# Splitting the last layer of a four-layer graph network: low nodes by buckets, high nodes by gathers

## The chip, the cores and the metric

The kernel runs on one core of a Trainium2 chip. The core has five engines that work from their own instruction streams: PE (TensorE, matmuls), DVE (VectorE), ACT (ScalarE), POOL (GpSimd, here mostly the issuer of indirect DMAs) and SP (SyncE, here the issuer of the plain DMAs). The metric is the device time of one execution in microseconds; a time is the median of several executions. A profiled execution is one more, with its own time.

## The reference, cut to what matters

There are 12500 nodes with 128 values each and 200000 edges `src -> dst`. The edges come sorted by `dst`; `dst` is drawn as 12500 times the square of a uniform number, so that low nodes have many edges and high nodes few: 121410 of the 200000 edges end in nodes below 4608. `src` is uniform. Four layers follow each other, each on a normalized copy `h` of the nodes and each added to them: an attention over all edges (layer 0), a second attention with edge weights (layer 1), and

```python
row = concatenate([src, dst]); col = concatenate([dst, src])     # layer 2: both directions
y = segment_sum(dinv[row] * dinv[col] * (h @ W)[col], row, N) + dinv**2 * (h @ W) + b

neigh = segment_sum(h[src], dst, N) / maximum(deg, 1)            # layer 3: into dst only
z = h @ W_self.T + neigh @ W_neigh.T + b
z = relu((z - mean(z, axis=0)) * rsqrt(var(z, axis=0) + 1e-5) * gamma + beta)
x = x + z
```

Layer 3 ends with a normalization over all nodes, so its mean and variance need every node's sum first.

## The kernel before, in words

Nodes lie in 98 blocks (`NB`) of 128. Tables that edges read (`zt` for layer 2, `h3` for layer 3) hold each row as two half-precision parts, 512 B, in DRAM.

The kernel sums along edges in two ways.

*By gathers.* A list holds, per edge, the row to fetch and the place in its block. `gather` (L291) issues one indirect DMA on POOL for 128 edges. A "hot" matrix, built by one DVE comparison (L1522), then adds the 128 fetched rows to their places by two matmuls (one for each part, L1524), and DVE adds the result to an accumulator (L1528). Layer 0 (`layer0_edges`, L1103) does this along `dst`, where the list needs no padding: 391 windows (`NW`) of 512 edges, each touching two neighbouring blocks, with a mask for each of the two. Its lists (`lists`, L1813) live in SBUF until layer 0 is over. Layers 1 and 2 do it along `src`, with lists padded to whole blocks: 1664 gathers each, in 416 groups of four (`sum_rows`, L1507).

*By buckets.* The second direction of layer 2, and the whole of layer 3, are summed along `dst` from edges sorted by block of `src` and, within a block, by class of `dst`. A class is `dst % 26` (`CLASSES`), its columns are `dst // 26` (`COLS` = 481, `COLS2` = 482). A bucket is one block and one class, at most 128 edges; there are 2548. `buckets` (L840) takes four classes at once (`AT_ONCE`) and walks all 98 blocks. For each block DVE builds `mine` (L867), which picks the source rows of 4x128 edges; for each bucket PE multiplies it with the block's table rows `z` (256 columns, L873), ACT copies the result `r` to half precision (L878), DVE builds `yours` (L875), the edges' columns within the class, and PE adds into the class's sums (two matmuls of 482 columns, L852). Two buckets make a step; a step's sums are added two steps later. `z` and the edges' lanes are loaded by SP for seven blocks at a time (`ZB`), in two buffers. When the four classes are through, `finish` is called for each. In layer 2 (`class_rows`, L891) it turns the sums by PE, copies them (`turned`, L904, two buffers) and stores them to the table `y` in DRAM. In layer 3 it multiplies with `W_neigh` (L1687), scales by the node's degree (`rdegk`, L1689), adds into `yt`, which holds all nodes turned (L1691), and takes the statistics (L1692).

The buckets' edges and columns are prepared beside layer 1 by `bucket_starts` (L749). It counts, for each bucket (128 in a column, `BC` = 20 columns), the edges before it, first over the first edges of all rows in five parts (L777), then within one row that it gathers (L790). It then gathers 128 edges (L805) from a view that starts at every fourth edge (`STEP`), finds which belong to the bucket and stores lanes and columns. Should a bucket not fit, `over` is set, the buckets are emptied, and loops that otherwise run no times (`sum_again`, `means_again`) gather all edges instead. The order of edges is made beside layer 0 by a sort whose keys are packed and unpacked by DVE (L373, L388).

The order of the work is that of the program, arranged by the framework within each engine's stream. In layer 2, `sum_rows` takes the bucket steps between its groups, 1300 of them over 416 groups. In layer 3 nothing but the buckets runs in the loop, with `own_parts` (`h @ W_self`, L1657) between: one of its 75 pieces at every second step. After the loop come the normalization and the output, L1698 on.

Of the kernel before, what the change touches and what calls it, by code (L numbers as in the profile page):

```python
# [36 lines left out]
P = 128  # L37
# [32 lines left out]
CLASSES = 26  # L70
COLS = -(-N // CLASSES)
COLS2 = COLS + COLS % 2
BUCKETS = NB * CLASSES
BC = -(-BUCKETS // P)

STEP = 4
# [30 lines left out]
class Net:  # L107
# [256 lines left out]
    def by_class(self, q, r, n):  # L364

        nc = self.nc
        nc.vector.tensor_scalar(q, n, 1.0 / CLASSES, 0.5 / CLASSES, op0=OP.mult, op1=OP.add)
        nc.vector.scalar_tensor_tensor(r, q, -float(CLASSES), n, op0=OP.mult, op1=OP.add)
        nc.vector.scalar_tensor_tensor(q, r, 0.0, q, op0=OP.is_ge, op1=OP.add)
        nc.vector.tensor_scalar(q, q, -1.0, None, op0=OP.add)  # L370
        nc.vector.scalar_tensor_tensor(r, q, -float(CLASSES), n, op0=OP.mult, op1=OP.add)

    def pack_buckets(self, key, own, other, more):  # L373
# [7 lines left out]
        self.by_class(own, more, other)  # L381
# [6 lines left out]
    def unpack_buckets(self, own, other, more, key):  # L388
        nc = self.nc
        ki = key.bitcast(I32)  # L390
        nc.vector.tensor_scalar(own, ki, 14, 0x3F80, op0=OP.logical_shift_right, op1=OP.bitwise_and)
        nc.vector.tensor_scalar(more, ki, P - 1, None, op0=OP.bitwise_and)
        nc.vector.tensor_tensor(own, own, more, op=OP.bitwise_or)
        nc.vector.tensor_scalar(other, ki, 7, 0x1FF, op0=OP.logical_shift_right, op1=OP.bitwise_and)
        nc.vector.tensor_scalar(more, ki, 16, 0x1F, op0=OP.logical_shift_right, op1=OP.bitwise_and)
        nc.vector.scalar_tensor_tensor(other, other, float(CLASSES), more, op0=OP.mult, op1=OP.add)

# [351 lines left out]
    def bucket_starts(self, work, take, keys, firsts, shifted, lanes, places, over):  # L749
# [6 lines left out]
        n = work.tile([P, BC], I32, name="bnum")  # L756
        nc.gpsimd.iota(n, pattern=[[P, BC]], base=0, channel_multiplier=1)
        s, k = (work.tile([P, BC], I32, name=f"b{c}") for c in "sk")
        self.by_class(s, k, n)
        nc.vector.tensor_scalar(s, s, 5, None, op0=OP.logical_shift_left)  # L760
        nc.vector.tensor_tensor(s, s, k, op=OP.bitwise_or)
# [9 lines left out]
        for h in range(5):  # L771
# [3 lines left out]
            for c in range(BC):  # L775
                below = work.tile([P, quarter], F32, name="bbelow")
# [20 lines left out]
        at = work.tile([P, BC], I32, name="bat")  # L797
        nc.vector.tensor_scalar(at, ri, int(math.log2(STEP)), None, op0=OP.logical_shift_right)
# [3 lines left out]
        for c in range(BC):  # L802
            m = min(P, BUCKETS - c * P)
            edge = work.tile([P, P], I32, name="bedge", bufs=2)
            self.gather(edge, shifted, at, c)  # L805
# [34 lines left out]
    def buckets(self, work, psum, table, lanes, place, finish):  # L840
# [14 lines left out]
        for k0 in range(0, CLASSES, AT_ONCE):  # L855
            n = min(AT_ONCE, CLASSES - k0)
            sums = [psum.tile([P, 512], F32, name=f"sums{i}", bufs=1)[:, :COLS2] for i in range(n)]
            for s in range(NB):
                if s % ZB == 0:
                    z = work.tile([P, ZB, PARTS * D], STORED, name="z", bufs=2)  # L860
                    nc.sync.dma_start(z, view[:, s:s + ZB, :])
                    lane = work.tile([P, ZB, AT_ONCE * P], F16, name="lanes", bufs=2)
                    nc.sync.dma_start(lane[:, :, :n * P], bass.AP(
                        tensor=lanes.tensor, offset=lanes.offset + (s * CLASSES + k0) * P,
                        ap=[[0, P], [CLASSES * P, ZB], [1, n * P]]))
                mine = work.tile([P, AT_ONCE * P], F16, name="mine", bufs=3)
                nc.vector.tensor_scalar(mine[:, :n * P], lane[:, s % ZB, :n * P], self.lane, None, op0=OP.is_equal)  # L867
                for i in range(0, n, 2):
                    p = psum.tile([P, 2, PARTS * D], F32, name="pout", bufs=2)
                    yours = work.tile([P, 2, COLS2], F16, name="yours", bufs=5)  # L870
                    for j in range(2):
                        b = s * CLASSES + k0 + i + j
                        nc.tensor.matmul(p[:, j, :], mine[:, (i + j) * P:(i + j + 1) * P], z[:, s % ZB, :],  # L873
                                         start=True, stop=True)
                        nc.vector.tensor_scalar(yours[:, j, :], self.iotac, place[:, b:b + 1], None,  # L875
                                                op0=OP.is_equal)
                    r = work.tile([P, 2, PARTS * D], F16, name="r", bufs=4)
# [7 lines left out]
            for i in range(n):  # L885
                o = work.tile([P, COLS2], F32, name="o", bufs=2)
# [4 lines left out]
    def class_rows(self, work, psum, out):  # L891

        nc = self.nc
        zero = work.tile([P, D], F32, name="zero")
        nc.vector.memset(zero, 0.0)
        nc.sync.dma_start(out[COLS * CLASSES:NP, :], zero[:NP - COLS * CLASSES, :])

        def finish(k, i, o):
            p = psum.tile([P, 4, P], F32, name="pout", bufs=2)
            t = work.tile([P, 4, P], F32, name="turned", bufs=2)  # L900
            for j in range(4):
                m = min(P, COLS - j * P)
                nc.tensor.transpose(p[:m, j, :], o[:, j * P:j * P + m], self.ident)
                nc.vector.tensor_copy(t[:m, j, :], p[:m, j, :])  # L904
                nc.sync.dma_start(bass.AP(tensor=out.tensor, offset=out.offset + (j * P * CLASSES + k) * D,
                                          ap=[[CLASSES * D, m], [1, D]]), t[:m, j, :])
# [28 lines left out]
    def windows(self, pool, psum, dram, lists, own, other, relb):  # L935
# [40 lines left out]
        some = pool.tile([P, 1], F32, name="somefar")  # L976
        nc.vector.tensor_reduce(some, far.rearrange("p a c -> p (a c)"), axis=AX.X, op=OP.add)
        p = self.bank(psum)
        nc.tensor.matmul(p[:, 0:1], self.ones, some, start=True, stop=True)
        nc.vector.tensor_scalar(self.sparse, p[:, 0:1], 0.5, None, op0=OP.is_gt)  # L980
# [585 lines left out]
    def layer2_edges(self, dram, zt, acc, edges, dbins, sbins, lanes, places, over):  # L1566
# [7 lines left out]
        with tc.tile_pool(name="l2a", bufs=1) as work, tc.tile_pool(name="ps22", bufs=1, space=PSUM) as psum:  # L1574
            once = self.count_of(work, over, 1)
# [35 lines left out]
    def layer3_table(self, dram, keep, x, chunks):  # L1611
# [9 lines left out]
        by_class = dram.tile([CLASSES, COLS2], F32, name="rdegc")  # L1621
        with tc.tile_pool(name="l3t", bufs=1) as pool, tc.tile_pool(name="ps3t", bufs=1, space=PSUM) as psum:
# [5 lines left out]
            t = pool.tile([CLASSES, COLS2], F32, name="rc")  # L1628
            nc.vector.memset(t, 0.0)
            nc.sync.dma_start(t[:, :COLS], bass.AP(tensor=by_node.tensor, offset=by_node.offset,  # L1630
                                                   ap=[[1, CLASSES], [CLASSES, COLS]]))
# [12 lines left out]
    def layer3(self, keep, x, table, dbins, lanes, places, over):  # L1644
# [5 lines left out]
        classes = yt.rearrange("p b e -> p (b e)")[:, :COLS * CLASSES].rearrange("p (j c) -> p j c", c=CLASSES)  # L1650
        with tc.tile_pool(name="l3a", bufs=1) as work, tc.tile_pool(name="ps33", bufs=1, space=PSUM) as psum:
            self.means_again(work, psum, yt, rdeg, ht_, dbins, over)
        st = keep.tile([P, CLASSES, 6], F32, name="bst")
        with tc.tile_pool(name="l3d", bufs=1) as work, tc.tile_pool(name="ps30", bufs=1, space=PSUM) as psum:
            place = self.bucket_places(work, places, over)

            def own_parts():  # L1657

                for lo, hi in GROUPS:
                    k = hi - lo  # L1660
                    h = work.tile([P, 4, D], F32, name="h", bufs=2)
# [4 lines left out]
                    p = psum.tile([P, 4, P], F32, name="ph")  # L1666
# [11 lines left out]
            rd = [None]  # L1678

            def finish(k, i, o):  # L1680
                if i == 0:
                    rd[0] = work.tile([P, AT_ONCE, COLS2], F32, name="rdegk")
                    n = min(AT_ONCE, CLASSES - k)
                    nc.sync.dma_start(rd[0][:, :n, :].rearrange("p k j -> p (k j)"),
                                      self.rows(by_class[k:k + n, :], n * COLS2))
                p = psum.tile([P, 512], F32, name="py")
                nc.tensor.matmul(p[:, :COLS2], self.wneigh, o, start=True, stop=True)  # L1687
                m = work.tile([P, COLS2], F32, name="m", bufs=2)
                nc.vector.tensor_mul(m, p[:, :COLS2], rd[0][:, i, :])  # L1689
                v = classes[:, :, k]  # L1690
                nc.vector.tensor_add(v, v, m[:, :COLS])  # L1691
# [3 lines left out]
            for i, _ in enumerate(self.buckets(work, psum, ht_, lanes, place, finish)):  # L1695
                if i % 2:
                    next(parts, None)
# [259 lines left out]
```

## Time and profile before

| | us |
|---|---|
| median of three timed runs | 8606.02 |
| lowest and highest of them | 8601.07 and 8621.12 |
| the profiled execution | 8595.46 |
| its span, first to last instruction | 8593.7 |
| busy in the span: PE / DVE / ACT / POOL | 6491.9 / 6414.5 / 4345.9 / 5029.4 |
| first and last start of a layer 2 gather | 4858.3 and 6984.6 |
| layer 3, from the clearing of `yt` to the last statistics | 7143.9 to 8563.65 |

In the profile, a digit in a row of slices is the busy share of one fortieth of the span (215 us) in tenths. Layer 0 takes the first ten slices, layer 1 the next twelve, layer 2 the next ten, layer 3 the last seven. A group's line names the line of the program, the engine, the operation, output and inputs, shape and count; then busy time and mean duration, and the idle time before it with what ended it. A wait's line names who waited for whom, the total in us, the number of times and the longest. In the list by time, an entry with "x4" is four instructions in a row, and the time after the first is that of all of them. Durations of matmuls overlap, so starts are better to count by than durations.

### The profile page before, as it was taken

The page shows a single profiled execution, that of the slowest core. Times are in us where ns is not written, and L with a number is a line of the kernel's source. Part 1 is how long each engine was busy: PE and PEld are TensorE (multiplying, and loading weights), DVE is VectorE, ACT ScalarE, POOL GpSimd, SP SyncE. Part 2 cuts the span into 40 slices and gives each one's busy share as a digit, 9 for nine tenths or more (in the row PEclk, how much of TensorE's full clock was granted, in tenths as well). Part 3 has the DMA queues.
Part 4 walks back from the last instruction along what each step waited for, and adds up shares of the span by engine and source line. Part 5 has one row for each costly group of instructions (what it writes and reads, how often), then busy time and mean ns, then how long its engine had stood idle before and what let it go on. Part 6 is the DMA issues. An engine that isn't in the chain of part 4 may idle for free. (4 is left out here: it accounts for less than half of the span.)

```text
span 8593.7 us, 134716 instructions
## 1 busy us (share of the span) xinstructions
PE 6491.9 (76%) x36173; PEld 4569.0 (53%) x36174; DVE 6414.5 (75%) x21784; ACT 4345.9 (51%) x8435; POOL 5029.4 (59%) x5224
## 2 busy tenths in 40 slices
PE   4455555555588988889995478888888767999999
PEld 3344444444377877778884244444444434555555
DVE  5788888887777776776777877777777776777777
ACT  4566666665455555555553333333333336555555
POOL 1777777777477777777774677777777731000000
PEclk7556655555766566665565699999999988999999
DMA  4333333333555555555553233444444443333333
GB/s 113 78 81 82 82 82 82 81 83 87 157 180 178 173 174 174 175 171 177 176 180 84 80 111 113 114 113 116 113 114 115 114 115 91 94 98 95 100 97 112
DMA packets 854249, 1021.59 MB, mean 119 GB/s; under 512 B 127765, under 2 KB 692914, under 8 KB 853232
## 3 DMA queue, kind: packets, MB, share of 16 engines
q1 hardware_dynamic: 637669, 558.29, 22.5%
q0 software_dynamic: 185728, 439.20, 18.7%
q10 hardware_dynamic: 30091, 15.25, 0.7%
q8 instruction: 319, 5.23, 0.2%
q14 instruction: 442, 3.62, 0.1%
HBM read 952.03 MB, written 60.29 MB: 118 GB/s over the span
## 5 line engine op out<-in xcount | busy, mean ns | idle before, releaser
L852 PE MATMUL sums<-yours,r 128*128 128x482 f16 x10192 | 2525.9, 372 | 219.4 <-ACT r L878 161.5
L878 ACT ACTIVATE r<-pout 128x512 f16<-128x512 f32 x2548 | 1474.0, 596 | 1941.8 <-PE pout L873 1935.9
L292 POOL DMA_INDIRECT rows<-kvt,idxs x1664 | 1618.7, 973 | 548.5 <-issue 420.9
L875 DVE TENSOR_SCALAR yours<-iotac,bucketp 128x482 f16<-128x482 f16 x5096 | 1646.1, 358 | 379.9 <-PE sums L852 379.1
L292 POOL DMA_INDIRECT rows<-zt,idxs x1664 | 1620.5, 974 | 511.2 <-issue 407.8
L292 POOL DMA_INDIRECT rows<-hw,idxd x1564 | 1489.0, 952 | 658.8 <-issue 380.9
L852 PEld LDWEIGHTS <-r 128*128 128x128 f16 x10192 | 963.2, 99 | 1032.2 <-ACT r L878 392.2
L1147 PE MATMUL psum<-rows,weights 128*128 128x130 f32 x3128 | 777.5, 419 | 589.5 <-ACT weights L1142 543.7
L1321 PE MATMUL psum<-weighted,hot 128*128 128x137 f32 x3328 | 942.8, 433 | 140.4 <-DVE acc L1323 70.7
L1147 PEld LDWEIGHTS psum<-rows,weights 128*128 128x128 f32 x3128 | 660.0, 307 | 671.5 <-ACT weights L1142 616.1
L873 PE MATMUL pout<-z,mine 128*128 128x256 f16 x5096 | 918.0, 276 | 14.1 <-DVE mine L867 9.1
L1321 PEld LDWEIGHTS psum<-weighted,hot 128*128 128x128 f32 x3328 | 732.3, 295 | 300.3 <-DVE acc L1323 196.3
L1528 DVE TENSOR_TENSOR acc<-acc,psum 128x128 f32 x1664 | 464.8, 279 | 493.7 <-PE psum L1524 487.2
L1281 ACT ACT_TABLE_LOAD x206 | 264.3, 1283 | 934.0 <-DMA near<-lengths 934.0
L873 PEld LDWEIGHTS <-mine 128*128 128x128 f16 x5096 | 478.3, 98 | 450.0 <-DVE mine L867 58.1
L1142 ACT ACTIVATE weights<-off,weight,minus 128x128 f32<-128x128 bf16 x1173 | 499.6, 483 | 386.0 <-DVE rows L1134 354.1
L1323 DVE TENSOR_TENSOR acc<-acc,psum 128x137 f32 x1664 | 486.6, 292 | 254.2 <-PE psum L1321 245.9
L1290 PE MATMUL pb<-we,near 128*128 128x8 f32 x3328 | 617.4, 322 | 3.0 <-ACT near L1281 3.0
L1290 PEld LDWEIGHTS pb<-we,near 128*128 128x128 f32 x3328 | 601.6, 279 | 20.3 <-issue 3.1
L867 DVE TENSOR_SCALAR mine<-lanes,lane 128x512 f16<-128x512 f16 (+1 forms) x1372 | 478.1, 350 | 3.1 <-PE pout L873 3.0
L1524 PE MATMUL psum<-rows,hot 128*128 128x128 f16 x3328 | 293.4, 221 | 217.7 <-DMA rows<-zt,idxs 214.5
L1316 DVE TENSOR_TENSOR weighted<-rows,weighted 128x512 f32<-128x512 f32 x416 | 271.4, 690 | 247.5 <-ACT weighted L1311 246.5
(461 smaller groups left out, 9506.2 us busy)
## 6 DMA issues: line engine op xcount, KB each, us to landing
lanes<-lanes SPq DMA_DIRECT2D x168, 896.0 KB
near<-lengths SPq DMA_DIRECT2D x208, 512.0 KB
lanes<-slanes SPq DMA_DIRECT2D x208, 256.0 KB
lanes<-dlanes SPq DMA_DIRECT2D x391, 128.0 KB
z<-zt SPq DMA_DIRECT2D x98, 448.0 KB
z<-h SPq DMA_DIRECT2D x98, 448.0 KB
rows<-kvt,idxs POOLq DMA_INDIRECT x1664
rows<-zt,idxs POOLq DMA_INDIRECT x1664
```

What stands on the lines that cost most here:

```text
L292: self.nc.gpsimd.indirect_dma_start(out=out, out_offset=None, in_=table, in_offset=bass.IndirectOffsetOnAxis(ap=idx[:, t:t + 1], axis=0))
L852: nc.tensor.matmul(sums[i], self.part(r[:, i, :], h), yours[:, i, :], start=s == 0 and h == 0, stop=s == NB - 1 and h == PARTS - 1)
L867: nc.vector.tensor_scalar(mine[:, :n * P], lane[:, s % ZB, :n * P], self.lane, None, op0=OP.is_equal)
L873: nc.tensor.matmul(p[:, j, :], mine[:, (i + j) * P:(i + j + 1) * P], z[:, s % ZB, :], start=True, stop=True)
L875: nc.vector.tensor_scalar(yours[:, j, :], self.iotac, place[:, b:b + 1], None, op0=OP.is_equal)
L878: nc.scalar.activation(r, p, AF.Copy)
L1142: nc.scalar.activation(hot[:, j, :], off, AF.Relu, bias=w[:, j:j + 1], scale=minus[:, j:j + 1])
L1147: nc.tensor.matmul(p, hot[:, j, :], rows[:, j, :n], start=j == 0, stop=j == G - 1)
L1290: nc.tensor.matmul(pb[:, j, :], hid[:, j * P:(j + 1) * P], self.we2, start=False, stop=j == W - 1)
L1321: nc.tensor.matmul(p, hot[j // G][:, j % G, :], v[:, j, :], start=True, stop=True)
L1323: nc.vector.tensor_add(d, d, p)
L1528: nc.vector.tensor_add(d, d, p[:, j, :])
```

## The change

1. There are 32 classes instead of 26, 16 (`FEW`) for nodes below 4608 (`SPLIT`) and 16 for those from 4608 on. A low class has 288 columns, a high one 496. Packing and unpacking of the sort's keys follow; there are 3136 buckets in 25 columns.
2. Layer 2 uses all 32 classes. Its `turned` tile has one buffer.
3. Layer 3's buckets are the 16 low classes only. Edges into higher nodes are gathered, from the last 155 (`LATE`) of layer 0's windows, whose lists are stored to DRAM after layer 0's preparation and loaded again in layer 3 (`late_sums`). Their sums go into an accumulator of 64 blocks from block 34 on (`BELOW` = 2 blocks of margin), which is cleared first. One late group of four gathers is taken at every fifth step, an own part at every fourth. After the loop, 16 groups of four blocks are scaled, turned, multiplied with `W_neigh` and added to `yt`, with statistics.
4. In layer 3, `z` and lanes are loaded two blocks at a time, in three buffers; `mine`, `yours`, `r`, `o`, `m`, `h` each have one buffer less, the scale row is loaded class by class into one buffer, and one PSUM tile (`py`) serves the own parts, the classes and the late groups.
5. A guard `early` joins `over`: it is set where the edge before the late windows already belongs to a node from 4608 on, or where a window was too wide.
6. A bucket's edges are read from its first edge on, not from the last multiple of four before it.

```diff
-CLASSES = 26
-COLS = -(-N // CLASSES)
-COLS2 = COLS + COLS % 2
+FEW = 16
+SPLIT = 36 * P
+CLASSES = 2 * FEW
+COLS = (SPLIT // FEW, (NP - SPLIT) // FEW)
+LATE = 155
+BELOW = 2
-STEP = 4
...
     def pack_buckets(self, key, own, other, more):
-        self.by_class(own, more, other)
+        nc.vector.tensor_scalar(own, other, int(math.log2(FEW)), None, op0=OP.logical_shift_right)
+        nc.vector.tensor_scalar(more, own, float(COLS[0]), float(FEW), op0=OP.is_ge, op1=OP.mult)
+        nc.vector.scalar_tensor_tensor(own, more, -COLS[0] / FEW, own, op0=OP.mult, op1=OP.add)
+        nc.vector.tensor_scalar(other, other, FEW - 1, None, op0=OP.bitwise_and)
+        nc.vector.tensor_tensor(more, more, other, op=OP.add)
...
     def unpack_buckets(self, own, other, more, key):
-        nc.vector.scalar_tensor_tensor(other, other, float(CLASSES), more, op0=OP.mult, op1=OP.add)
+        nc.vector.scalar_tensor_tensor(other, other, float(FEW), more, op0=OP.mult, op1=OP.add)
+        nc.vector.tensor_scalar(more, more, float(FEW), float(SPLIT - FEW), op0=OP.is_ge, op1=OP.mult)
+        nc.vector.tensor_tensor(other, other, more, op=OP.add)
...
     def bucket_starts(...):
-        at = work.tile([P, BC], I32, name="bat")
-        nc.vector.tensor_scalar(at, ri, int(math.log2(STEP)), None, op0=OP.logical_shift_right)
-            self.gather(edge, shifted, at, c)
+            self.gather(edge, shifted, ri, c)
...
-    def buckets(self, work, psum, table, lanes, place, finish):
+    def buckets(self, work, psum, table, lanes, place, finish, classes=CLASSES, zb=ZB):
+        for k0 in range(0, classes, n):
+            cols = COLS[k0 // FEW]
+                if s % zb == 0:
+                    some = 2 + (zb < ZB)
+                    z = work.tile([P, zb, PARTS * D], STORED, name="z", bufs=some)
...
     def class_rows(self, work, psum, out):
-            t = work.tile([P, 4, P], F32, name="turned", bufs=2)
+            t = work.tile([P, 4, P], F32, name="turned")
...
+    def late_sums(self, work, psum, table, lists, yt, rdeg, st):
+        acc = work.tile([P, NB - low, D], F32, name="late")
+        nc.gpsimd.memset(acc, 0.0)
+        for g in range(LATE):
+            lo = g * G
+            rows = work.tile([P, G, PARTS * D], STORED, name="rows", bufs=4)
+            for j in range(G):
+                self.gather(rows[:, j, :], table, idx, lo + j)
+            b = self.blocks_of(slot, g, 1, [DVE], NB - low - 2)
+            p = psum.tile([P, D], F32, name="psum", bufs=1)
+            for j in range(G):
+                hot = work.tile([P, P], PART, name="hot", bufs=4)
+                nc.vector.tensor_scalar(hot, self.iotac[:, :P], place[:, lo + j:lo + j + 1], None, op0=OP.is_equal)
+                for h in range(PARTS):
+                    nc.tensor.matmul(p, hot, self.part(rows[:, j, :], h), start=j == 0 and h == 0,
+                                     stop=j == G - 1 and h == PARTS - 1)
+            d = acc[:, bass.ds(b[0], 2), :]
+            for i in range(2):
+                nc.vector.scalar_tensor_tensor(d[:, i, :], p, mask[:, g, i:i + 1], d[:, i, :], op0=OP.mult, op1=OP.add)
+            yield
+        for i, (lo, hi) in enumerate(groups(SPLIT // P, NB)):
+            k = hi - lo
+            p = psum.tile([P, 512], F32, name="py")[:, :k * P].rearrange("p (b e) -> p b e", e=P)
+            for j in range(k):
+                a = acc[:, lo + j - low, :]
+                nc.scalar.activation(a, a, AF.Copy, scale=rdeg[:, lo + j:lo + j + 1])
+                nc.tensor.transpose(p[:, j, :], a, self.ident)
+            t = work.tile([P, 4, P], F32, name="hT", bufs=2)
+            nc.scalar.activation(t[:, :k], p, AF.Copy)
+            p = psum.tile([P, 512], F32, name="py")[:, :k * P].rearrange("p (b e) -> p b e", e=P)
+            nc.tensor.matmul(p, self.wneigh, t[:, :k], start=True, stop=True)
+            v = yt[:, lo:hi, :]
+            nc.vector.tensor_add(v, v, p)
+            nc.vector.bn_stats(st[:, i, :], v.rearrange("p b e -> p (b e)")[:, :min(hi * P, N) - lo * P])
+            yield
...
             def finish(k, i, o):
-                if i == 0:
-                    rd[0] = work.tile([P, AT_ONCE, COLS2], F32, name="rdegk")
+                rd = work.tile([P, COLS[0]], F32, name="rdegk")
+                nc.sync.dma_start(rd, self.rows(by_class[k:k + 1, :], COLS[0]))
...
-            for i, _ in enumerate(self.buckets(work, psum, ht_, lanes, place, finish)):
-                if i % 2:
+            sums = self.late_sums(work, psum, ht_, late, yt, rdeg, st[:, FEW:, :])
+            taken = 0
+            for i, _ in enumerate(self.buckets(work, psum, ht_, lanes, place, finish, FEW, 2)):
+                if i % 4 == 1:
                     next(parts, None)
+                while taken * 5 < i and taken < LATE:
+                    next(sums)
+                    taken += 1
+            for _ in parts:
+                pass
+            for _ in sums:
+                pass
...
+    late_lists = [dram.tile(shape, dtype, name=f"late{i}") for i, (shape, dtype) in enumerate(
+        (([P, LATE * G], I32), ([P, LATE * G], F32), ([P, LATE, 2], F32), ([1, LATE], I32)))]
+    for t, f in zip(late_lists, (lists[0][:, (NW - LATE) * G:NW * G], lists[1][:, (NW - LATE) * G:NW * G],
+                                 lists[3][:, NW - LATE:, :], lists[4][:, NW - LATE:])):
+        nc.sync.dma_start(t, f)
-    shifted = bass.AP(tensor=skeys.tensor, offset=skeys.offset, ap=[[STEP, (R + 1) * P // STEP], [1, STEP]])
+    shifted = bass.AP(tensor=skeys.tensor, offset=skeys.offset, ap=[[1, (R + 1) * P], [1, 1]])
```

## The prediction

> **What bounds the kernel now.** I read the page first (span, slices, groups), then the table by stretches for the last two layers, then the instructions in order of time inside them, then the waits. The profiled execution took 8595.46 us (span 8593.7); the median of the three timed runs is 8606.02, so 10.6 us are added at the end.
>
> The page's slices, and the two stretches of layer 2 (first line) and layer 3 (second), with time, then busy us of PE, weight load, DVE, ACT, POOL, granted clock, DMA share and GB/s:
>
> ```profile
> PE   4455555555588988889995478888888767999999
> POOL 1777777777477777777774677777777731000000
> 4900.00:6950.00 2050.00, 1644.31 (x10609) 883.91 (x10607) 1515.73 (x6364) 695.70 (x1245) 1561.48 (x1604) 0.96 0.41 115
> 7170.00:8550.00 1380.00, 1363.75 (x7777) 766.25 (x7776) 1013.40 (x3309) 804.85 (x1390) 25.12 (x20) 1.00 0.33 96
> ```
>
> Layer 3 is TensorE and nothing else: 1363.75 of 1380 us at clock 1.00, POOL idle. Layer 2 is POOL: 76% busy looks like slack, but the instructions in order of time show a gather every 1.25 us, the 0.30 us between two being "issue", with little else in it:
>
> ```profile
> 6001.24 0.94 POOL L292 DMA_INDIRECT rows<-zt,idxs  x1 [0.30 <-issue]
> 6002.49 0.94 POOL L292 DMA_INDIRECT rows<-zt,idxs  x1 [0.30 <-PE psum L1524]
> 6003.74 0.94 POOL L292 DMA_INDIRECT rows<-zt,idxs  x1 [0.30 <-issue]
> ```
>
> 1664 gathers from 4858.3 to 6984.6 make 1.279 us each, 5.11 per group of four. TensorE in that stretch works 80% (4.10 us per group) and waits 165 us for rows, so its own pace with its other waits is 92% of 5.11, 4.70 us:
>
> ```profile
> PEld L852 <- ACT r L878: 366.6, 484, 1.1
> PE psum L1524 <- DMA rows<-zt,idxs: 165.2, 147, 5.4
> PE sums L852 <- ACT r L878: 154.8, 331, 0.8
> ```
>
> The unit prices of layer 3, from the bucket loop in order of time: one step (two buckets: two gathers by matmul of 256 columns, four sums of 482) starts at 7446.21 and the next at 7447.25.
>
> ```profile
> 7446.21 0.38 PE L873 MATMUL pout<-z,mine 128*128 128x256 f16 x2
> 7446.43 0.98 PE L852 MATMUL sums<-yours,r 128*128 128x482 f16 x4
> 7447.25 0.38 PE L873 MATMUL pout<-z,mine 128*128 128x256 f16 x2
> 7447.46 0.98 PE L852 MATMUL sums<-yours,r 128*128 128x482 f16 x4
> ```
>
> That is 1.033 us for 2440 columns, 0.423 ns a column. Class groups of four end at 7400.9 and 7610.3: 209.4 us, of which 196 steps are 202.5 and the hand-over 7.
>
> **The change part by part.**
>
> *Layer 3's buckets.* 2548 buckets of 482 columns become 1568 (16 classes by 98 blocks) of 288. A step has 512+4x288=1664 columns: 0.704 us. 784 steps: 552 us. Four hand-overs: 28 us by the row above. The copies o, m and the scale rows rdegk get one buffer each, so each class's scale row can be fetched only once the one before is used; that is bounded by nothing (fetched in time) and 5 us a class (the y store below took 5 us from last copy to landing); I take 2, 32 us in all. The product that waits for the row stands on DVE ahead of the next group's selections, so PE feels it. ScalarE's copies (L878, 0.50 us apart where two follow) fit in 0.70.
>
> *Layer 3's late gathers.* 155 groups: 620 gathers by 1.279, 793 us, plus the 25 POOL additions of the own parts, 1.3 us each: 826 us of POOL. TensorE: eight 128-column matmuls a group, 0.61 us by the L1524 rows: 95 us; own parts 46 us (18.4+27.5, rows L1668 and L1673); scaling 16 matmuls, 10 us. TensorE in all: 552+60+95+46+10=763 us, 4.92 per group; with the 0.6 us of cross-waits that a group has in layer 2 (4.70-4.10) 5.5, 855 us. DVE: a step two selections of 288 and half a selection of 512 (0.26 us apart for 482, so about 0.21 and 0.26), 0.55 us, 431 in all; late 155x(4x0.16+2x0.27)=183; rest 70: 684, below both. So POOL and TensorE come out almost level, 826 and 855, and I take 870 for their meeting. Ends: 826, and 1000 (the cross-waits of 0.6 tripled, 6.5 us a group).
>
> *Its ends.* Before: the clearing of yt, 10.55 us at 7143.9, is waited for; the second clearing (64 of 98 blocks) adds 6.9. After the last gather: 5 us to land and multiply (the first gather of layer 2 took 6.7). Then 16 groups of transposes, copy, matmul, add through one PSUM buffer, which wait for the whole accumulator. The same chain for the own parts ran at 3.6 us a group with two buffers (copies at 7157.01, 7160.60, 7164.21); with one 3.8, 61 us; ends 45 and 75. Layer 3 now: 10.6+6.9+870+5+61=953 us, against 7143.9 to the last statistics at 8563.65, 1420: **-467** (-527 to -323).
>
> *Loads cut from 7 blocks to 2.* 1344 KB per seven become 384 KB per two, 196 pairs, three buffers. Layer 3 moved 115.31 MB at 32.7% of the engines in 1200 us, so full speed is 294 KB per us: 1.3 us a pair, with 210 KB of gathers 2.0 of the 4.4 us that four steps last. Two pairs ahead hide a landing up to 8.8 us. Nearest row of a landing: the first loads of layer 3 were issued at 7155.1 and used at 7166.3, 11.2 us, but with some 4 MB ahead of them. I take nothing; price in the rivals.
>
> Here the skill speaks against the change. The Trainium skill, "DMA: Bandwidth & Descriptors", section Bandwidth, says to batch transfers to 1 MiB or more, and its section Anatomy of one DMA has about 2.0 us fixed for each. By those figures a pair costs an estimated 2.9 us; hidden it changes nothing, bare it would add 196x2.9=568 us and turn the sign. No row of this case shows a bare small load.
>
> *Layer 2.* 3136 buckets for 2548; 1600 steps over the same 416 gather groups, 3.85 for 3.125. First half (288 columns): TensorE needs about 2.7 us of steps for 3.2, so POOL stays the bound, no change. Second half (496 columns, 2496 a step, 1.056 us): 3.77 bucket steps by 1.056 = 3.98 for 3.07x1.033=3.17, +0.81 a group. Work alone 4.10+0.81=4.91 still fits under 5.11; own pace 4.70+0.81=5.51 doesn't: 208x0.40=+83. That such a pace is real is seen where the gathers run out, at the end of layer 2: there the groups start 5.3 us apart with no wait for rows.
>
> ```profile
> 6994.23 0.61 PE L1524 MATMUL psum<-rows,hot 128*128 128x128 f16 x8
> 6999.52 0.61 PE L1524 MATMUL psum<-rows,hot 128*128 128x128 f16 x8
> 7004.82 0.61 PE L1524 MATMUL psum<-rows,hot 128*128 128x128 f16 x8
> ```
>
> The turned rows lose their second buffer: each class waits for the store of the one before; the third class's first copy at 5198.56 followed the first's last at 5193.2 by 5 us, waiting for that store. Three such waits at each of eight hand-overs; behind them on DVE stand the additions to acc and the next selections, which PE awaits. POOL runs seven groups ahead (35 us) and covers them inside the layer; without that cover 8x15=120 us. At the layer's end, bare, 12 us. **+95** (0 to +184).
>
> *Layer 1.* Ten more gathers (25 columns of buckets for 20, twice) on POOL, the bound there in most slices: 10x1.279=**+13** (0 to 25). DVE gets 25 more counts of 0.62 us, hidden (it is 72% busy). The gathers from the first edge on read rows of one element as start; with rows of four they took 944 ns, with rows of 128 also 944: nothing.
>
> *Layer 0 and seams.* Two more operations on 1664 columns after the sort (1.02 and 1.89 us, rows L395 and L393), between layers and bare: +3. Five operations of the packing become five. Four stores of lists, 0.36 us of SP each, ahead of the first lane loads, and four flag operations of 0.15: +1. **+4** (0 to 10). The clearings that go (rc 0.46, zero) stand beside DMA waits: nothing.
>
> Another rule against it, without use in the sum: the Trainium skill's "GPSIMD Engine Reference", section Key points, says that GpSimd shares SBUF interfaces with VectorE and contends with DVE's two-port modes. If no gather could run beside layer 3's selections, 431 us would join POOL's 826, and the time be 8250+(1257-870)=8637. The layer 2 stretch has DVE 74% and POOL 76% busy at once, and gathers of 974 ns mean against 952 in layer 0, so the trace does not show such a block.
>
> **Sum.** -467+95+13+4=-355; 8595.5-355=8240, and 10.6 up to the median: **8250 us**.
>
> **The rivals.**
> - *Bound everywhere by POOL.* Layer 3 loop 826, short tail, layer 2 unchanged: -527+0+13+4: 8096. For it: TensorE's work alone fits in both. Against: its waits for ACT r.
> - *Cross-waits in layer 3.* Every late group puts eight matmuls and two PSUM additions between the steps, on single buffers; at 6.5 us a group the loop is 1000, and layer 2 +150: 8435. For it: the 5.3 us groups above.
> - *Loads late (ends on the other side).* If pairs land 11.2 us after issue, they come 2.4 us late, 196 times: +470, 8720. It decides from 6.2 us a pair, where the loop reaches 1220. Against it: 45% load, less than layer 1's 57%.
> - *It doesn't do what it says.* If the guards fire, all edges are gathered again, over 2000 us more in each layer. By the inputs the last edge ahead of the late windows has node 4561, under 4608, and the fullest bucket 125 of 128, so they don't.
>
> **How the numbers follow.** Main case 0.70 (8130 to 8400), POOL-bound 0.13, cross-waits 0.11, loads late 0.05, guards 0.01. The range 8120 to 8440 leaves out a part of the first and the last two. A change under 0.2% (17 us) can't be told from none; only the last two are slower, about 0.01 lies between.
>
> **What would show it.** Layer 3's stretch about 950 us with POOL about 76% busy; sums of 288 columns, steps 0.70 us apart; groups of hot matmuls 5.1 to 5.6 us apart. In layer 2's second half POOL's gathers pause (a wait for PE psum over 0.3 us) and PE is over 90% busy. DVE waits for y stores several us, 24 times. Wrong if SP's loads are what mine waits for in layer 3, or if layer 2's halves are equally long.

## The result, and the profile after

The changed kernel takes 8853.3 us (median of four runs, 8846.93 to 8858.64), the kernel before, run beside it, 8605.97 (8601.07 to 8621.12): 1.0284 times as long, 95% interval 1.0266 to 1.0302. The prediction was 8250 us, faster. It is wrong by sign, and the profile says where. The page's slices of the changed kernel:

```profile
POOL 1777777775577677777765555555555555447772
PEclk7556555555766666666555778888898899879997
DMA  5333333334555555555551454445555545557784
```

Its stretches of layer 2, of layer 3's loop and of the tail behind it (columns as before):

```profile
4950.00:7650.00 2700.00, 1889.24 (x12526) 1104.85 (x12524) 1618.32 (x7155) 858.69 (x1559) 1574.21 (x1619) 0.86 0.53 98
7900.00:8700.00 800.00, 665.95 (x5575) 521.15 (x5574) 649.86 (x2705) 464.15 (x827) 591.27 (x604) 0.94 0.76 139
8750.00:8818.00 68.00, 46.15 (x88) 17.63 (x88) 19.83 (x29) 8.74 (x15) 0.00 (x0) 0.50 0.00 0
```

Layer 3 did shrink: from the clearing of `yt` (7833.1) to the last statistics it takes 986 us, where it took 1420. What was lost lies in layer 2, for which the prediction had given +95. Its gathers, 4911.6 to 7681.3, take 2770 us for 2126, +643, and POOL, busy 76% of it before, is busy 58%. The engines of the DMA are busier (0.53 for 0.41) and move less (98 GB/s for 115). The waits in that stretch:

```profile
DVE acc L1531 <- PE psum L1527: 977.7, 351, 12.8
POOL rows L296 <- DMA rows<-zt,idxs: 673.0, 192, 8.9
PE psum L1527 <- DMA rows<-zt,idxs: 522.3, 151, 11.6
```

POOL waited 56.1 us in all for earlier gathers to land, 0.3 at most; now 673.0, up to 8.9 at a time. The instructions in order of time show one such stop:

```profile
5403.10 0.36 SPq L860 DMA_DIRECT2D lanes<-lanes  x1
...
5403.94 0.36 SPq L858 DMA_DIRECT2D z<-zt  x1
...
5411.14 0.94 POOL L296 DMA_INDIRECT rows<-zt,idxs  x1 [0.30 <-issue]
5412.39 0.94 POOL L296 DMA_INDIRECT rows<-zt,idxs  x1 [0.30 <-issue]
5421.98 0.59 PE L1527 MATMUL psum<-rows,hot 128*128 128x128 f16 x4 [10.66 <-DMA rows<-zt,idxs]
...
5422.19 0.94 POOL L296 DMA_INDIRECT rows<-zt,idxs  x1 [8.86 <-DMA rows<-zt,idxs]
```

SP issues one load of lanes and one of z, the gathers behind them stay on their way until 5422, and with their buffers POOL stops, then TensorE. Loads of lanes were issued at 5016.66, 5041.20, 5062.53, 5086.95 and 5111.23: every 21 to 25 us the same. The DMA queues tell what these loads cost (packets, MB, share of all sixteen engines). Of the kernel before, in the 2000 us from 4900 on:

```profile
q1 hardware_dynamic: 173179, 123.80, 22.4%
q0 software_dynamic: 50014, 102.53, 17.8%
```

Of the changed kernel, in the 2700 us from 4950 on:

```profile
q1 hardware_dynamic: 211146, 155.68, 39.2%
q0 software_dynamic: 51712, 106.01, 13.2%
```

The gathers' queue q0 costs per MB what it did (356 us of share for 102.53 MB, 356 for 106.01). SP's queue q1 took 448 us for 123.80 MB and now takes 1058 for 155.68: 3.6 us a MB became 6.8. Divided by the pairs of loads issued in those windows (88, 110), a pair took 5.1 us of all sixteen engines and takes 9.6. Packets per MB are nearly the same (1399, 1356). By the traces' records of single packets on q1, during layer 2's gathers, only the loads of lanes grew: their packets of 1024 B took 60 ns on average before and take 141, those of 512 B, z's among them, 28 in both.

No line of the diff is about these loads; CLASSES changes them. A load of lanes reads, for each of seven blocks, the 1 KB of four classes, all 128 partitions the same bytes. The rows of lanes lie CLASSES x 128 x 2 bytes apart: with 26 classes 6656 B, with 32 classes 8192 B.

### The profile page after: what moved, and what is told of

Same layout as the page of the kernel before. It is cut to its first block, busy times and chain, and to the rows that moved or that the text cites. A ratio compares the mean times of both kernels' runs of the same rounds, so it can differ in the third digit from the quotient of the medians.

```text
span 8850.0 us, 136359 instructions
## 1 busy us (share of the span) xinstructions
PE 6128.6 (69%) x36324; PEld 4607.6 (52%) x36325; DVE 6231.7 (70%) x22235; ACT 4219.7 (48%) x8318; POOL 5648.3 (64%) x5855
## 5 line engine op out<-in xcount | busy, mean ns | idle before, releaser
L875 ACT ACTIVATE r<-pout 128x512 f16<-128x512 f32 x2352 | 1331.3, 596 | 2095.7 <-PE pout L870 2040.3
L847 PE MATMUL sums<-yours,r 128*128 128x288 f16 (+1 forms) x9408 | 1953.4, 335 | 200.0 <-ACT r L875 119.3
L872 DVE TENSOR_SCALAR yours<-iotac,bucketp 128x288 f16<-128x288 f16 (+1 forms) x4704 | 1373.1, 325 | 69.4 <-PE sums L847 67.4
L847 PEld LDWEIGHTS <-r 128*128 128x128 f16 x9408 | 903.7, 103 | 778.9 <-ACT r L875 395.8
L870 PE MATMUL pout<-z,mine 128*128 128x256 f16 x4704 | 871.7, 292 | 54.7 <-ACT r L875 28.9
L1527 PE MATMUL psum<-rows,hot 128*128 128x128 f16 x3328 | 334.3, 230 | 591.6 <-DMA rows<-zt,idxs 583.1
L296 POOL DMA_INDIRECT rows<-h,late x620 | 601.4, 970 | 220.7 <-issue 144.9
L1293 PE MATMUL pb<-we,near 128*128 128x8 f32 x3328 | 638.2, 328 | 3.0 <-ACT near L1284 3.0
L1293 PEld LDWEIGHTS pb<-we,near 128*128 128x128 f32 x3328 | 623.6, 287 | 20.2 <-issue 3.1
L1527 PEld LDWEIGHTS <-hot 128*128 128x128 f16 x3328 | 248.9, 101 | 698.4 <-issue 610.9
```

Source lines behind the costliest of these rows:

```text
L296: self.nc.gpsimd.indirect_dma_start(out=out, out_offset=None, in_=table, in_offset=bass.IndirectOffsetOnAxis(ap=idx[:, t:t + 1], axis=0))
L847: nc.tensor.matmul(sums[i], self.part(r[:, i, :], h), yours[:, i, :], start=s == 0 and h == 0, stop=s == NB - 1 and h == PARTS - 1)
L872: nc.vector.tensor_scalar(yours[:, j, :], self.iotac[:, :cols], place[:, b:b + 1], None, op0=OP.is_equal)
L875: nc.scalar.activation(r, p, AF.Copy)
L1293: nc.tensor.matmul(pb[:, j, :], hid[:, j * P:(j + 1) * P], self.we2, start=False, stop=j == W - 1)
L1527: nc.tensor.matmul(p[:, j, :], hot, self.part(rows[:, j, :], h), start=h == 0, stop=h == PARTS - 1)
```

## The experiments

**The distance alone, both ways.** Theory A: the distance of 8192 B makes the loads slow, and they hold up the gathers. Rivals: more to load (B), hand-overs and wider sums (C). The first run pads the rows; the other three put the old kernel's rows 8192 B apart, keep a group's lanes in one run, and double the distance. The main lines of the edits are shown; in before_8192 and group_lanes the stores of the lanes are split into smaller ones to fit.

```
+PITCH = (CLASSES + 1) * P        # pad_lanes; before_8192: 32 * P; pitch_16384: 2 * CLASSES * P
-   nc.sync.dma_start(lanes[c * P:(c + 1) * P, :], lane)
+   nc.sync.dma_start(bass.AP(tensor=lanes.tensor, offset=lanes.offset + c * P // CLASSES * PITCH,
+                             ap=[[PITCH, P // CLASSES], [P, CLASSES], [1, P]]), lane)
-       offset=lanes.offset + (s * CLASSES + k0) * P, ap=[[0, P], [CLASSES * P, zb], [1, n * P]]
+       offset=lanes.offset + s * PITCH + k0 * P,     ap=[[0, P], [PITCH, zb], [1, n * P]]
...
# group_lanes: the four classes of a group together, all blocks in a row
+RUN = AT_ONCE * P
...
+       offset=lanes.offset + (k0 // n * (BC * P // CLASSES) + s) * RUN, ap=[[0, P], [1, zb * RUN]]
```

> The changed kernel with one block of empty space behind each block's row of lanes in DRAM: rows 8448 B apart instead of 8192 B; nothing else differs. Theory A (the row pitch of 8192 B makes the broadcast loads of lanes slow, and these hold up the gathers on the same 16 engines): layer 2's gathers take 2126 to 2230 us again instead of 2770, q1 moves its bytes in layer 2 at about 276 MB per ms of full share instead of 147, the kernel ends at 8200 to 8320. Rival B (there is more to load: 112 pairs of loads instead of 98, 156 MB instead of 124): no change, 8853 within 20. Rival C (the single buffer `turned` and the wider class sums hold up layer 2): no change, 8853 within 20.

> The kernel before with its rows of lanes put 8192 B apart instead of 6656 B; nothing else differs but the stores of the lanes, cut at the rows (6 small ones in place of one, 20 times in layer 1). Theory A: it becomes slower, by about 98/112 of 643 = 560 us in layer 2 and by 100 to 560 in layer 3, whose 98 pairs are the same: 9250 to 9730 in all. Rivals B and C: 8606 within 30.

> The changed kernel with the lanes of one group of four classes kept together in DRAM, so that a load reads 7 KB in one run (2 KB in layer 3) where it read pieces of 1 KB 8192 B apart; the bytes and the loads are the same. Theory A: as the run with padded rows or better, 8150 to 8320. Rivals B and C: 8853 within 20. If the padded rows help but this doesn't, it is not the pitch but the number of different addresses read at once.

> The changed kernel with the rows of lanes 16384 B apart. Theory A in its strict form (a large power of two is slow, whichever): 8853 or slower, up to 9300. If only the distance of 8192 B itself were slow: 8200 to 8320. Rivals B and C: 8853 within 20.

Measured, the kernel before being 8601.18 us on that chip:

| run | us | ratio to before (95%) | layer 2's gathers | layer 3 |
|---|---|---|---|---|
| pad_lanes (8448 B) | 8298.62 | 0.9656 (0.9637 to 0.9676) | 2248 | 949 |
| before_8192 | 9163.83 | 1.0653 (1.0635 to 1.0671) | 2646 | 1488 |
| group_lanes (one run) | 8205.96 | 0.9539 (0.9523 to 0.9555) | 2139 | 950 |
| pitch_16384 | 8729.42 | 1.0153 (1.0136 to 1.0170) | 2669 | 967 |

256 empty bytes behind each row take 555 us off the changed kernel (8853.3, beside a kernel before of 8605.97); 8192 B put into the old kernel cost 563. B and C fall as causes of the loss: bytes, loads, the single buffer and the sums are the same in all runs of the changed kernel. Three expectations were missed: before_8192 stays below its 9250 (reason below), pitch_16384 lies between the two times named for it, and pad_lanes moves 189 MB per ms of full share on q1, not 276. SP's queue and the gathers of pad_lanes, in the 2200 us from 4950 on and over the whole run:

```profile
q1 hardware_dynamic: 210912, 155.44, 37.3%
L298 POOL DMA_INDIRECT rows<-zt,idxs x1664 | 1619.8, 973 | 633.8 <-issue 413.0 <-DMA rows<-zt,idxs 163.3 <-PE pout L873 35.8
```

And of group_lanes, in the 2100 us from 4950 on and over the whole run:

```profile
q1 hardware_dynamic: 127200, 155.44, 22.6%
L298 POOL DMA_INDIRECT rows<-zt,idxs x1664 | 1622.1, 975 | 522.6 <-issue 428.8 <-PE pout L875 39.7 <-DMA rows<-zt,idxs 28.3
```

The waiting for gathers goes from 680 us (changed kernel) to 163 and 28. A pair of loads takes 7.5 us with 8448 B and 4.4 in one run: padding by 256 B takes away 2.1 of the 5.2 us between 9.6 and 4.4.

In before_8192 layer 3 shows what it means that loads are hidden behind other work. Its pairs cost 8.7 us of the engines there (59.2% of 1400 us for 95) instead of 4.7, yet its class groups end 209.4 us apart as before, since TensorE needs longer than the 14 pairs of a group (122 us). Only the last group, of two classes, grows, from 109 to 172 us.

**Which part of the distance.** Theory A2: what counts is how far the pieces of one load coincide when their places are counted around 8192 B. Rival D: any rows more than 8 KB apart are slow. Two runs test this; beside them stand the old kernel with its lanes in one run, and another order of layer 3's closing steps (below).

> The changed kernel with rows of lanes 9216 B apart (8192 + 1024): counted around 8192 B, the seven pieces of 1 KB of one load lie at 0, 1, 2 ... 6 KB, where a distance of 8448 B puts them at 0, 256, 512 ... 1536 B and one of 8192 B all at 0. Theory A2 (what counts is how many different places, around 8192 B, a load's pieces take): a pair of loads takes 4.4 to 5.1 us of all sixteen engines, as with 6656 B or with the lanes in one run, instead of 7.5 (8448 B) or 9.6 (8192 B); layer 2's gathers 2140 to 2190 us, the kernel 8205 to 8250. Rival D (any pieces further apart than 8 KB are slow, whatever the remainder): 8299 within 20, as with 8448 B.

> The changed kernel with rows of lanes 12288 B apart (8192 + 4096): around 8192 B the pieces lie at 0 and 4 KB by turns. Theory A2: two places instead of one, so between 8192 B and 8448 B: 8400 to 8750. Rival D: 8299 to 8730, no order by the remainder. If only powers of two are slow: 8205 to 8250.

> The kernel before with the lanes of one group of four classes kept together, as in the run of the changed kernel with that layout. With pieces 6656 B apart its pair of loads takes 5.1 us of all engines, and in one run it should take 4.4: its gathers wait 57.9 us for earlier rows in layer 2, and at most that goes, so 8545 to 8600. Then the change itself, with the layout equal on both sides, is worth 340 to 395 us (8206 against this run), where the prediction's steps made it 355. Rival: this layout helps before by as much as it helps the changed kernel (647 us), so that the change is slower on equal terms: under 8206.

> The changed kernel with the lanes in one run, and the 16 closing steps of layer 3's late part (each scales, turns and multiplies four blocks) taken inside the loop over buckets, at 23 of 5 steps, instead of after it. If the 74 us of the tail are waiting of one engine for the next, the loop hides most of it and pays only their matmuls, some 30 us, on a TensorE that is 84% busy: 8150 to 8190. If the loop is bound by TensorE or by the gathers so tightly that all comes back there: 8206 within 10.

These four ran on a chip on which the kernel before takes 10366 us: 10249, 10228, 10437 and 10266, ratios 0.989, 0.987, 1.007 and 0.990. Their times decide nothing (last section), but the cost of a pair can be read there: 4.6 us with 9216 B and 6.0 with 12288. Three of them and group_lanes were then run on another chip, and two more distances beside the kernel before again.

> The changed kernel with rows of lanes 9216 B apart, once more, since the chip of the first look ran the kernel before at 10366 us instead of 8601, with engines standing still for nothing that the profile shows, and so could not tell times of layers apart. There a pair of loads took 4.6 us of all engines with 9216 B. Theory A2: layer 2's gathers 2140 to 2190 us on a chip that runs before at 8600, the kernel 8205 to 8250. Rival D: 8299 within 20, as with 8448 B.

> The kernel before with the lanes in one run for each group of classes, once more for the same reason. 8545 to 8600 where before runs at 8601; the rival (the layout helps before as much as the changed kernel): under 8206.

> The changed kernel with the lanes in one run and the 16 closing steps of layer 3's late part inside the loop over buckets, once more for the same reason. 8150 to 8190 if the tail was waiting that the loop hides; 8206 within 10 if all comes back in the loop.

> The changed kernel with the lanes in one run, once more, beside the three others on one chip: 0.954 of the time before, within 0.003, where the chip runs before at 8601.

> The changed kernel with rows of lanes 8704 B apart (8192 + 512). So far a pair of loads in layer 2 took, in us of all sixteen engines: 9.6 (8192), 8.8 (16384), 7.5 (8448), 6.0 (12288), 5.1 (6656, the kernel before), 4.6 (9216), 4.4 (one run); in layer 3, where a load has two pieces of 1 KB: 2.42 (8192), 2.19 (8448), 1.38 (9216 and 12288), 1.39 (one run). If what counts is how far the pieces overlap when their places are counted around 8192 B: here two pieces overlap by half, so 1.8 to 2.0 in layer 3, and the seven cover 4 KB, so 5 to 6.5 in layer 2 and 8210 to 8260 in all. If the places are cells of 512 B or less, 1.4 in layer 3 and 4.6 in layer 2; if cells of 1 KB with nothing in between, 1.8 to 2.4.

> The changed kernel with rows of lanes 10240 B apart (8192 + 2048). Around 8192 B the seven pieces lie at 0, 2, 4, 6, 0, 2 and 4 KB, four places where 12288 B gives two and 9216 B seven; the two pieces of a load of layer 3 lie apart. By the number of places: 1.4 us a pair in layer 3, 4.6 to 6.0 in layer 2, 8190 to 8240 in all. If the turn is not 8 KB but 4 KB: two places, 6.0 as with 12288 B (which would then have had one, and does not fit); if it is 16 KB or more: seven places, 4.6.

Before was 8591.35 us beside the first four and 8588.9 beside the last two: pitch_9216_b 8192.88 (0.9535, 0.9520 to 0.9551), before_group_b 8595.50 (1.0008, 0.9999 to 1.0018), group_spread_b 8192.80 (0.9536, 0.9520 to 0.9552), group_lanes_b 8191.09 (0.9537, 0.9521 to 0.9553), pitch_8704 8213.15 (0.9564, 0.9536 to 0.9591), pitch_10240 8203.14 (0.9552, 0.9524 to 0.9580). A distance of 9216 B is as good as one run, so D falls (the kernel's time lies 12 us under the range expected). The distances in the order of their price, with the us of all sixteen engines that a pair takes (share by window, by pairs):

| distance, B | pieces around 8192 B | pair in layer 2 | pair in layer 3 (two pieces) |
|---|---|---|---|
| 8192 | all at 0 | 9.6 | 2.42 |
| 16384 | all at 0 | 8.8 | 2.22 |
| 8448 | 256 B on | 7.5 | 2.19 |
| 12288 | 0 and 4 KB by turns | 6.0 | 1.38 |
| 8704 | 512 B on | 5.1 | 1.96 |
| 10240 | 0, 2, 4, 6 KB | 5.0 | 1.36 |
| 9216 | 1 KB on | 4.6 | 1.38 |
| one run | | 4.4 | 1.36 to 1.39 |

The right column is the clearest. With two pieces of 1 KB that coincide wholly a pair costs 2.42 us (2.22 with 16384 B), by three quarters 2.19, by half 1.96, not at all 1.36 to 1.39, wherever the second one lies (1, 2 or 4 KB on, or next to the first). This column also speaks for a turn of 8192 B against its neighbours: were it 4 KB, pieces 12288 B apart would coincide (1.38); were it 16 KB, pieces 8192 B apart would not (2.42). Not all is explained. Why 16384 B is somewhat cheaper than 8192 B stays open, and so does how seven pieces add up: by the number of places 12288 B, with two, was expected between 8192 and 8448 B, and it is cheaper than both. The lines of layer 3 behind the first and the last row (800 us from 7900 on in the changed kernel):

```profile
q1 hardware_dynamic: 98674, 71.90, 53.8%
```

and group_lanes_b, in the 770 us from 7280 on:

```profile
q1 hardware_dynamic: 76227, 72.24, 31.5%
```

What in the memory turns around 8 KB no run shows. The Trainium skill, "DMA: Bandwidth & Descriptors", section Latency and other measured facts, has a loss of this kind for row pitches of 512 KiB to 8 MiB, down to half the rate, and gives the aliasing of memory channels as an inference, not verified. Here a loss appears at 8 KiB, where 128 partitions read the same pieces; whether it has the same reason no run shows.

**What the change is worth on equal terms.** The rival in the expectation of before_group_b, that the layout helps both kernels alike, falls: before gains nothing (1.0008). Its 6656 B spread the pieces already: the pair falls only from 5.1 to 4.3 us, and POOL waited 0.3 us at most for rows before. With lanes in one run on both sides the change makes 8595.50 into 8191.09, -404 us.

**The closing steps.** The loop over buckets takes them in:

```
-                while taken * 5 < i and taken < LATE:
-                    next(sums)
+                while taken * 23 < 5 * i and taken < LATE + len(groups(SPLIT // P, NB)):
+                    next(sums)
```

The time is that of group_lanes_b (8192.80 and 8191.09): the rival was right. From the last class group's first copy the end is 14 us away instead of 86, but from the first late gather to that copy it is 911 us instead of 843.

## Why the prediction was wrong, and where it was right

The step that failed is the sentence on layer 2's first half: "First half (288 columns) ... so POOL stays the bound, no change". It weighs TensorE against POOL and has no term for SP's loads, which stood at nothing in all of layer 2. The runs show 608 us in its place: so much longer is layer 2, from the first gather to the clearing of `yt`, in the changed kernel (2921.5 us) than in group_lanes (2313.3), where only the place of the lanes and the stores that put them there differ. Behind it stands an assumption that the part on loads spells out for layer 3, a price per byte carried over to the new layout: "full speed is 294 KB per us: 1.3 us a pair". There a pair took 2.42 us in the changed kernel, and 1.36 to 1.39 with the lanes in one run; the price was nearly right for pieces that lie apart. I had counted the pieces, bytes and issues of the new loads and not their addresses: CLASSES is also the stride of a tensor in DRAM. The test that I had named did fire: "Wrong if ... layer 2's halves are equally long". Its class groups take 346 to 355 us in the first half and 340 to 347 in the second.

Step by step, on equal terms (before_group_b and group_lanes_b, where pitch_9216_b agrees with the latter):

- *Layer 3, -467 predicted:* 1419.4 to 950.6 us, -468.8. In the changed kernel as it stands -434, since its loads are slow there too. That the sum fits so well is luck: two of its terms are off by 50 and 44 us and cancel. From the first late gather to the end of the last it is 820 us, where 870 was given for the loop: POOL's end of the range (826) held, the cross-waits did not bind. The end after the last gather is 110 us where 66 were given: the rest of the last bucket group and its four closings take 36, and the 16 closing groups 74 for 61. These stand 4.7 us apart, where the prediction put 3.8 for one PSUM buffer, from the 3.6 us of the own parts with two. The clock is not what differs: it was 0.50 in the tail (stretches of the changed kernel, third line) and 0.50 also where the 3.6 us were read (kernel before, 7156 to 7166), and the matmuls are nearly as long. The stretch there and its instructions of TensorE, then those in the tail of group_lanes_b:

```profile
7156.00:7166.00 10.00, 7.85 (x18) 3.96 (x18) 5.48 (x11) 7.81 (x20) 5.06 (x4) 0.50 0.96 313
7159.50 1.06 PE L1668 MATMUL ph<-ident,h 128*128 128x128 f32 x4
7161.25 2.08 PE L1673 MATMUL py<-hT,wself 128*128 128x512 f32 x2 [0.69 <-ACT hT L1670]
7163.11 1.06 PE L1668 MATMUL ph<-ident,h 128*128 128x128 f32 x4
```

```profile
8089.51 1.11 PE L1690 MATMUL py<-ident,late 128*128 128x128 f32 x4 [0.78 <-DVE yt L1696]
8091.36 2.08 PE L1694 MATMUL py<-hT,wneigh 128*128 128x512 f32 x2 [0.74 <-ACT hT L1692]
8094.22 1.12 PE L1690 MATMUL py<-ident,late 128*128 128x128 f32 x4 [0.78 <-DVE yt L1696]
```

  From the product to the next group's transposes it is 1.86 us there and 2.86 here. There the transposes have a tile of their own, `ph`; here they write into the product's tile `py` and wait until DVE has read it: the term that was mis-sized is the second buffer, 1.0 us a group and not 0.2.
- *Steps and groups there:* the sums of 288 columns run at 0.71 us a step, 0.70 predicted, POOL at 77% in the loop. The instructions of TensorE in group_lanes_b, in order of time:

```profile
7600.04 0.38 PE L875 MATMUL pout<-z,mine 128*128 128x256 f16 x2
7600.26 0.65 PE L852 MATMUL sums<-yours,r 128*128 128x288 f16 x4
7600.75 0.38 PE L875 MATMUL pout<-z,mine 128*128 128x256 f16 x2
7600.97 0.65 PE L852 MATMUL sums<-yours,r 128*128 128x288 f16 x4
```

- *Layer 2, +95 (0 to 184):* from the first gather to the clearing of yt 2293 to 2315, +21. The rule of the two halves holds once the loads are cured (stretches of group_lanes_b):

```profile
4950.00:5930.00 980.00, 740.65 (x5972) 497.08 (x5971) 728.87 (x3414) 405.82 (x744) 744.17 (x774) 0.93 0.42 129
5950.00:7000.00 1050.00, 946.37 (x6062) 507.81 (x6063) 843.73 (x3477) 418.74 (x753) 792.62 (x804) 0.97 0.39 123
```

  TensorE is 90% busy in the second half, and its class groups take 279 us, for 263 in the first half. The old layer takes 2157 us from its first gather to its last class group. Against half of that, 1078, the second half takes 1116, +37, for which +83 was given, and the first 1055, -23, which I had not priced. The groups of hot matmuls stand 5.36 us apart on average in the second stretch and 5.08 in the first (1566 and 1544 matmuls, eight a group): slower than POOL's 5.11, as said, but short of the 5.51 given.
- *Stores of the turned rows:* covered, as said. DVE waits 12 times, 10.7 us in all; in the changed kernel, where the stores stand behind the slow loads, 16 times and 58.4 us.
- *Layers 0 and 1, +17 (0 to 35):* +40. Ten gathers make the 13 given, but layer 1's gathers also wait 12 us more for weighted and acc on DVE, so DVE's added work there is not wholly hidden; no run takes the 25 counts alone. Layer 0 gives +14 for the +4; I did not take that apart.
- *The rivals:* POOL-bound (8096) and cross-waits (8435) are both off. "Loads late" has the sign and SP's loads, but neither the place nor the mechanism: I sought it in layer 3, from the latency of small loads, and it came in layer 2 from the engines' time that large loads took. In the cured kernel the loop of layer 3 shows no wait for lanes or `z` (7240 to 8060 of group_lanes_b), so its loads of two blocks are hidden there. The guards did not fire.
- *The skill's rules named there:* the pair of small loads takes 1.36 to 1.39 us of the engines and is hidden, near the 1.3 from the trace and not the estimated 2.9 us by the page's figures. These are the page's for transfers issued by GpSimd, SP issues the ones here, and the estimate counts the fixed part once for two loads. Gathers and selections do run side by side in layer 3 (POOL 77% and DVE 85% of 770 us in group_lanes_b).

The sum on equal terms is -469+21+40=-408, by the spans -407, where the prediction had -355. The fall to 8853 is this and the loads: group_lanes took 8206 with the same work.

## What to carry to other kernels

When a constant changes, list every tensor in DRAM whose row it sets, and count where the pieces of one load then lie: here a pair of loads, with 1 KB pieces that all partitions read, took 9.6 us of the engines with the pieces 8192 B apart and 4.4 with them in one run. Whether loads whose partitions read different bytes show this was not run. Bytes and issues do not show it; the share of engine time per MB of the queue does, and one run per load (or a distance that spreads the pieces) cured it here. And a price per byte belongs to an access pattern: whoever carries it over to a new layout should bound it from both sides.

## What the runs showed of the hardware

- The step is gradual in the overlap: in layer 3 the first two quarters of a piece that no longer coincide save 0.23 us of a pair each (2.42, 2.19, 1.96), the last two together 0.6, and without overlap a pair costs what it costs in one run (1.36 to 1.39).
- Chips differ. On one of them the kernel before took 10365.59 us (10317.5 to 10389.77, eight runs), 1.2 times the others, and the changed kernel with 9216 B 10248.84 for 8192.88, 1.25 times. Instructions take as long there (a gather 970 ns, 973 elsewhere) and the loads cost the same; what grows is the time between them. The mean granted clock of TensorE is lower there too (0.695 for 0.735 with 9216 B). The gathers of layer 1 in pitch_9216 there:

```profile
L298 POOL DMA_INDIRECT rows<-kvt,idxs x1664 | 1613.4, 970 | 1327.1 <-DVE weighted L1322 802.4 <-issue 454.5 <-DVE acc L1329 47.2
```

and in pad_lanes on the first chip:

```profile
L298 POOL DMA_INDIRECT rows<-kvt,idxs x1664 | 1618.3, 973 | 569.3 <-issue 427.3 <-DVE weighted L1322 64.9 <-DVE acc L1329 29.0
```

  On that chip TensorE also stands for 391.2 us ahead of its weight loads of L873 in pitch_9216 with no releaser that the profile shows (58.3 in pad_lanes). Why, no run here shows; times from that chip were not compared with times from others for any result above.
